# A graph layer on one core: y of a block made from its own x and placed by a selection product, and the first five parts gathering rows of x while the table is built

## The chip, the core and the metric

The program runs on one core of one Trainium2 chip. A core has TensorE (PE; the loads of its stationary operand are listed apart as PEld), VectorE (DVE), ScalarE (ACT), GpSimd (POOL) and SyncE (SP). Each works through its own list of instructions in order; they wait for one another through semaphores. DMAs are issued here from SP, ACT and POOL. The metric is the device time of the whole program in microseconds (us), as the median of several executions.

## What is computed

```python
N, D = 12500, 128                      # nodes, features
E = 412500                             # edges, sorted by dst
theta = x[dst] - x[src]
w = sigmoid(relu(theta @ W1 + b1) @ W2 + b2)      # one weight per edge
agg = segment_sum(w * theta, dst, num_segments=N)
indeg = segment_sum(ones(E, 1), dst, num_segments=N)
gnn = agg + indeg * (x @ W4 + b4)
out = layernorm(x + gnn)               # eps 1e-5
```

All inputs and the output are fp32. With y = x W1, an edge needs relu(y[dst] - y[src] + b1); the sum w * (x[dst] - x[src]) needs the row x[src] as well.

## The kernel before

**The table.** For all nodes the kernel first computes y = x W1 and stores rows z = [y | x] of 256 numbers (1 KB) in DRAM. This loop (L122 to L142) runs over 14 chunks, 12 of them of 1024 nodes: load x (L127, ACT's queue), transpose 128 x 128 tiles on TensorE (L133), copy them to SBUF (L135), multiply by W1 (L138), copy y into the tile `zt` (L140), copy x beside it (L141), store `zt` to z (L142, SP's queue). `zt` has three buffers, `xt` six.

**The parts.** The edges are cut in parts of 1024 (8 tiles of 128 edges): 403 parts, the last with 7 tiles. For each tile POOL issues one indirect DMA that gathers the 128 rows z[src] into `zbuf` (L233); there are 3223 of them. `zbuf` has 7 buffers, and the gather of part s+4 stands in the program at part s. `src_i` holds the indices; it is made by loading the edge list, transposing it on TensorE and converting it (`place_src`, L297).

**The blocks.** Two parts make a block (202 blocks). The 96 nodes from the first dst of a block are its window; a part's own window is 41 nodes from the part's first dst. For each block SP loads x of the window (`xw`, L343) and, for each of its parts, the 41 rows y three times, one below the other, into `yw` (L336: six DMAs of 20.5 KB per block from z; `yw` has three buffers). Rows 123 to 125 of `yw` hold b1 in three pieces. `window` (L346) splits y into three bf16 pieces, so that a product in bf16 is exact enough: ACT L351 makes `yh`, ACT L352 copies `yw` into PSUM, DVE L353 and ACT L355 make the second piece, DVE L357 writes `y3`. It also transposes `xw` (PE L359, ACT L361 gives `xwT`).

**A part's work.** `one_hots`: TensorE copies the dst offset of every edge over all partitions (PE L372, into the single PSUM buffer `pd`, in two halves of 4 tiles), DVE L375 turns each half into a selection matrix `oh`, PE L379 multiplies it with `y3` and so puts y[dst] + b1 of every edge into PSUM (`ph`). DVE L382 builds the second selection matrix `ow` (edge to node of the window; two buffers). `weights`: DVE L393 subtracts y[src] out of `zbuf`, DVE L394 applies relu and the factor W2, DVE L398 sums to one number `lg` per edge, ACT L399 takes the sigmoid, and eight ACT instructions L401 scale the rows x[src] into `wx`. `add_up`: eight fp32 matmuls PE L419 add `ow`^T `wx` into the block's sum `pa`; before the first of them PE L415 brings over the sum of nodes shared with the block before. At a block's end `total` reads `pa` (ACT L439 into `a`), computes x W4 + b4 (PE L442 and L443) and the row of the layer norm (DVE L450 to L457), and `store` writes rows that are done (DVE L429, SP L430). Every eighth block the square root is taken for eight blocks at once (ACT L462, with a table load before it and one after).

**The order.** SP's instructions run as the program lists them (`manual_schedule`). On the other engines a scheduler has fixed the order when the kernel was built. For a block, counted from its first part, "even", and its second, "odd", VectorE's list before the change is: L393 odd; L382 odd; L450; L394 even; L451; L398 even; L453; L353; L375 (second half, next even); small ones; L375 (first half, next odd); L357; L382 next even; L394 odd; L375 (second half, next odd); L398 odd; L393 next even; L375; and then L393 of the next odd part.

Two small PSUM pools matter here: `ps_l` has one buffer each for `pd`, `pw` and `pa`, and `ps_h` has two for `ph`.

Of the kernel before, what the change touches and what calls it, by code (L numbers as in the profile page):

```python
# [30 lines left out]
LB = 8  # L31
EPS = 1e-5
# [3 lines left out]
def gnn_resnorm(  # L36
# [12 lines left out]
):  # L49

# [67 lines left out]

    with tc.tile_pool(name="tab", bufs=3) as tp, tc.tile_pool(
        name="tab_ps", bufs=2, space=bass.MemoryType.PSUM  # L120
    ) as tps:
        for n0, np_, m in chunks:  # L122
            def rows_of(t):
                return t[n0:n0 + np_ * m, :].rearrange("(p t) d -> p t d", t=m)

            xt = tp.tile([P, TC, D], F32, name="xt", bufs=6)
            nc.scalar.dma_start(xt[:np_, :m, :], rows_of(x))  # L127
            zt = tp.tile([P, TC, 2 * D], F32, name="zt")
            for g0 in range(0, m, G):
                g = min(G, m - g0)  # L130
                px = tps.tile([P, G, P], F32, name="tpx")
                for j in range(g):
                    nc.tensor.transpose(px[:, j, :np_], xt[:np_, g0 + j, :], ident[:np_, :np_])  # L133
                xT = tp.tile([P, G, P], F32, name="txT")
                nc.scalar.activation(xT[:, :g, :np_], px[:, :g, :np_], AF.Copy)  # L135
                py = tps.tile([P, G, D], F32, name="tpy")
                for j in range(g):
                    nc.tensor.matmul(py[:np_, j, :], xT[:, j, :np_], wts[:, 0, :],  # L138
                                     start=True, stop=True)
                nc.vector.tensor_copy(zt[:np_, g0:g0 + g, :D], py[:np_, :g, :])  # L140
            nc.scalar.activation(zt[:np_, :m, D:], xt[:np_, :m, :], AF.Copy)  # L141
            nc.sync.dma_start(rows_of(z), zt[:np_, :m, :])  # L142

    base_r = const.tile([1, NS], I32, name="base_r")
    with nc.allow_non_contiguous_dma(reason="each part's first dst"):
        nc.scalar.dma_start(
            base_r, bass.AP(tensor=dst.tensor, offset=dst.offset, ap=[[0, 1], [BE, NS]]))
    loaded.append(load(nc.scalar, dst, *sets[0]))
    nc.scalar.dma_start(wts[:, 1, :], W4)
    rows = {}  # L150
    for name, v in (("b4_r", b4), ("b1_r", b1), ("w2_r", W2)):
        rows[name] = const.tile([P, D], F32, name=name)
        nc.scalar.dma_start(
# [3 lines left out]
    nc.scalar.dma_start(b2_c, bass.AP(tensor=b2.tensor, offset=b2.offset, ap=[[0, P], [1, 1]]))  # L157
# [25 lines left out]
    y_f = fix[:, 2 * P:].rearrange("p (h d) -> p h d", h=SUB)  # L183
# [19 lines left out]
    nc.vector.scalar_tensor_tensor(place_c, ge[3], -4.0 * N, place_c, op0=OP.mult, op1=OP.add)  # L203
    b1_s = const.tile([P, D], F32, name="b1_s")
    bh = const.tile([P, D], BF16, name="bh")
    br = const.tile([P, D], F32, name="br")
    e_c = const.tile([P, 1], F32, name="e_c")
    nc.vector.tensor_copy(br, b1_r)
    nc.vector.memset(b1_s, 0.0)
    for lo, hi in zip([ge[3]] + eb[:2], eb):  # L210
        nc.vector.tensor_copy(bh, br)
        nc.vector.tensor_sub(e_c, lo, hi)
        nc.vector.scalar_tensor_tensor(b1_s, bh, e_c, b1_s, op0=OP.mult, op1=OP.add)
        nc.vector.tensor_sub(br, br, bh)

    yw_buf = [const.tile([P, SUB, D], F32, name=f"yw{i}") for i in range(3)]
    for t in yw_buf:
        nc.vector.memset(t, 0.0)
        for h in range(SUB):
            nc.vector.tensor_copy(t[96:, h, :], b1_s[96:, :])  # L220
# [10 lines left out]
    def gather(s):  # L231
        for k in range(tiles(s)):
            nc.gpsimd.indirect_dma_start(  # L233
                out=zbuf[s % NZ][:, k, :], out_offset=None, in_=z,
# [3 lines left out]
    base_s = const.tile([1, NS], I32, name="base_s")  # L238
# [81 lines left out]
    with tc.manual_schedule(engines={SP}), tc.tile_pool(name="work", bufs=2) as wp, tc.tile_pool(  # L320
# [163 lines left out]
        for s in range(min(AHEAD, NS)):  # L484
            gather(s)
# [215 lines left out]
```

## Time and profile before

| | |
|---|---|
| median of 10 runs | 4125.93 us (4121.54 to 4127.70) |
| the profiled execution | 4122.61 us, of which its span from the first to the last instruction is 4120.8 us |
| TensorE clock granted, mean over the span | 0.657 of full speed |
| busy: PE, PEld | 2567.9 us (62%), 2111.3 us (51%) |
| busy: DVE | 2812.6 us (68%) |
| busy: ACT | 1507.9 us (37%) |
| busy: POOL | 3049.0 us (74%) |
| DMA | 494.31 MB, mean 120 GB/s; 369 GB/s in the first 40 us |

A busy share is a mean over the span. Between 80 and 4090 us the kernel repeats itself every 20 us, one block at a time, so the shares say how full each engine is within a block, and the idle time before an instruction, with what ended it, says what that instruction waited for. Times in a timeline are us from the start of the span. In it, a row is one instruction or several of one line merged: start, duration, engine, line, operation, output<-inputs, shape, count, and in brackets the idle time of the engine before it with what ended it. Durations of matmuls are modelled, and an fp32 matmul leaves two records.

### The profile page before, as it was taken

What the parts mean: (1) busy time and instruction counts of PE and PEld (TensorE: products, weight loads), DVE (VectorE), ACT (ScalarE), POOL (GpSimd) and SP (SyncE); (2) the same over time, 40 slices, a digit from 0 to 9 for tenths busy, and PEclk for the clock granted to TensorE, in tenths of its full rate; (3) what the DMA queues carried; (4) which work ended last, traced back from release to release, by engine and by line L of the source; (5) the groups of instructions that cost most, each with busy time, mean ns of one, the idle gap of its engine ahead of it and who ended that gap; (6) DMA issues with size and microseconds to landing.
All of it is one profiled execution on the core that took longest, in us unless ns stands there. A gap on an engine that the chain in (4) does not pass through costs nothing.

```text
span 4120.8 us, 54409 instructions
## 1 busy us (share of the span) xinstructions
PE 2567.9 (62%) x14665; PEld 2111.3 (51%) x14665; DVE 2812.6 (68%) x4456; ACT 1507.9 (37%) x4782; POOL 3049.0 (74%) x3232
## 2 busy tenths in 40 slices
PE   5666656666656566566666666666566666666665
PEld 4555545545545445455555555555444555545554
DVE  5777667667667667666666676676676676676666
ACT  4343333333333333333333333333333333333333
POOL 3777777777777777777777777777777777777775
PEclk8666666667666676766676666666766666666665
DMA  7443444444444434444444444444344344444442
GB/s 267 116 118 114 121 116 115 119 116 117 118 114 120 117 113 121 116 114 121 116 115 119 117 116 117 116 119 118 113 120 117 113 122 116 114 120 116 116 119 85
DMA packets 257189, 494.31 MB, mean 120 GB/s; under 512 B 60441, under 2 KB 149858, under 8 KB 255336
## 3 DMA queue, kind: packets, MB, share of 16 engines
q0 software_dynamic: 154704, 422.65, 35.9%
q1 hardware_dynamic: 98284, 58.66, 4.8%
q10 hardware_dynamic: 3884, 9.44, 0.6%
q8 instruction: 118, 1.93, 0.2%
q14 instruction: 199, 1.63, 0.1%
HBM read 467.78 MB, written 22.73 MB: 119 GB/s over the span
## 4 chain that ended last, share of the span: by engine, by line
DVE 28%; DMA 28%; ACT 15%; PE 13%; issue 11%; POOL 4%; SPq 1%; DVEq 0%; ACTq 0%; POOLq 0%
DMA zbuf<-z,src_i 26%; ACT wx L401 12%; PE pa L419 11%; DVE lg L398 10%; DVE h L394 7%; DVE ow L382 5%; POOL zbuf L233 4%; ACT wx L399 3%; DVE oh L375 2%; DVE h L393 2%; PE pd L372 1%; DVE v L451 1%; DMA z<-zt 1%; DVE y L357 1%; DVE o L429 1%
## 5 line engine op out<-in xcount | busy, mean ns | idle before, releaser
L233 POOL DMA_INDIRECT zbuf<-z,src_i x3223 | 3047.9, 946 | 1042.8 <-issue 511.4
L419 PE MATMUL pa<-wx,ow 128*96 128x130 f32 x6446 | 1597.2, 414 | 206.6 <-ACT wx L401 188.0
L419 PEld LDWEIGHTS pa<-wx,ow 128*96 128x96 f32 x6446 | 1286.8, 259 | 444.4 <-ACT wx L401 363.6
L401 ACT ACTIVATE wx<-zbuf,wx 128x128 f32<-128x128 f32 x3223 | 988.3, 388 | 13.2
L375 DVE TENSOR_SCALAR oh<-pd,place_c,one_c 128x512 bf16<-128x512 f32 x806 | 646.3, 802 | 508.0 <-PE pd L372 508.0
L393 DVE TENSOR_TENSOR h<-ph,zbuf 128x1024 f32<-128x1024 f32 x403 | 491.1, 1219 | 534.5 <-DMA zbuf<-z,src_i 527.5
L372 PE MATMUL pd<-ident_b,off 128*128 128x128 bf16 x3223 | 668.8, 284 | 150.8 <-DVE oh L375 146.3
L415 PE MATMUL pa<-a,sh 96*96 96x130 f32 x402 | 130.3, 422 | 807.5 <-DVE v L451 806.5
L399 ACT ACTIVATE wx<-lg,b_c 128x8 f32<-128x8 f32 x403 | 124.1, 308 | 1366.7 <-DVE lg L398 1361.3
L415 PEld LDWEIGHTS pa<-a,sh 96*96 96x96 f32 x402 | 71.1, 231 | 860.4 <-issue 858.5
L394 DVE SCALAR_TENSOR_TENSOR h<-h,fix 128x1024 f32<-128x1024 f32 x403 | 486.9, 1208 | 0.0
L398 DVE TENSOR_REDUCE lg<-h 128x8 f32<-128x1024 f32 x403 | 486.9, 1208 | 0.0
L379 PE MATMUL ph<-y,oh 128*128 128x128 bf16 x3223 | 348.8, 274 | 213.9 <-DVE oh L375 213.7
L372 PEld LDWEIGHTS <-off 128*128 128x128 bf16 x3223 | 389.5, 136 | 107.3 <-issue 94.3
L382 DVE TENSOR_TENSOR ow<-fix,rel 128x768 f32<-128x768 f32 x403 | 383.1, 951 | 75.3 <-PE pa L419 75.2
L379 PEld LDWEIGHTS <-oh 128*128 128x128 bf16 x3223 | 278.2, 125 | 261.8 <-DVE oh L375 253.0
L352 ACT ACTIVATE fix<-yw 128x256 f32<-128x256 f32 x202 | 78.2, 387 | 593.3 <-DVE h L394 593.3
L351 ACT ACTIVATE yh<-yw 128x256 bf16<-128x256 f32 x202 | 82.7, 409 | 271.0 <-DMA yw<-z 271.0
L359 PE MATMUL pw<-ident,xw 96*128 96x96 f32 x202 | 85.0, 421 | 142.1 <-DVE v L453 129.3
L439 ACT ACTIVATE a<-pa 96x130 f32<-96x130 f32 x202 | 55.4, 274 | 313.4 <-PE pa L419 313.4
L429 DVE TENSOR_SCALAR o<-v,mv,sd 96x128 f32<-96x128 f32 x202 | 63.8, 353 | 125.3 <-DMA out_dram<-o 125.1
L359 PEld LDWEIGHTS pw<-ident,xw 96*128 96x128 f32 x202 | 36.7, 182 | 207.1 <-DVE v L453 193.4
(96 smaller groups left out, 1280.2 us busy)
## 6 DMA issues: line engine op xcount, KB each, us to landing
zbuf<-z,src_i POOLq DMA_INDIRECT x3223
yw<-z SPq DMA_DIRECT2D x1209, 20.5 KB
z<-zt SPq DMA_DIRECT2D x12, 1024.0 KB
xw<-in_x_dram SPq DMA_DIRECT2D x202, 48.0 KB
out_dram<-o SPq DMA_DIRECT2D x202, 48.0 KB
xt<-in_x_dram ACTq DMA_DIRECT2D x12, 512.0 KB
e_i<-in_dst_dram ACTq DMA_DIRECT2D x3, 512.0 KB
e_i<-in_src_dram ACTq DMA_DIRECT2D x2, 512.0 KB
```

The source lines that it names most:

```text
L233: nc.gpsimd.indirect_dma_start(out=zbuf[s % NZ][:, k, :], out_offset=None, in_=z, in_offset=IndirectOffsetOnAxis(ap=src_i[:, k, s:s + 1], ...
L372: nc.tensor.matmul(pd[:, j, :], off[:, k0 + j, s:s + 1].to_broadcast([P, P]), ident_b, start=True, stop=True)
L375: nc.vector.tensor_scalar(oh[:, k0:k0 + g, :], pd[:, :g, :], place_c, one_c, op0=OP.is_equal, op1=OP.max)
L379: nc.tensor.matmul(ph[:, k, :], oh[:, k, :], blocks[b]["y3"][:, h, :], start=True, stop=True)
L382: nc.vector.tensor_tensor(ow[:, :n, :], iota_f.to_broadcast([P, n, WB]), rel[:, :n, s:s + 1].to_broadcast([P, n, WB]), op=OP.is_equal)
L393: nc.vector.tensor_sub(h[:, :n, :], d["ph"][:, :n, :], zs[:, :n, :D])
L394: nc.vector.scalar_tensor_tensor(h[:, :n, :], h[:, :n, :], 0.0, w2_f.to_broadcast([P, n, D]), op0=OP.max, op1=OP.mult)
L398: nc.vector.tensor_reduce(lg[:, :n], h[:, :n, :], AX.X, OP.add)
L399: nc.scalar.activation(wx[:, :n, D], lg[:, :n], AF.Sigmoid, bias=b2_c)
L401: nc.scalar.activation(wx[:, k, :D], zs[:, k, D:], AF.Copy, scale=wx[:, k, D:D + 1])
L415: nc.tensor.matmul(bd["pa"][:WB], sh[:WB, :WB], carry[0][:WB], start=True, stop=False)
L419: nc.tensor.matmul(bd["pa"][:WB], d["ow"][:, k, :], wx_buf[s % 2][:, k, :], start=h == 0 and k == 0 and carry[0] is None, stop=end and k = ...
```

## The change

Y of a block's window is no longer loaded. TensorE multiplies the transposed `xw` by W1 (new L360, into the PSUM tile `pw`), ACT copies the result to SBUF (`yb`, L362; rows 96 to 98 hold b1's three pieces, written once), and for each of the two parts a selection matrix `pick` (DVE L367, from the constants `behind` and `far`) puts the rows at their places in a product (PE L370, into `pw`). From there `yh`, `y1`, `ym`, `y3` follow as before, reading PSUM. The loads L336 and their register loads go.

Parts 0 to 4 (`NH = 5`) gather rows of x, not of z, into the x half of `zbuf`, so they need no table; their y[src] is computed in `both`: transposes of the gathered rows, and a product with -W1 on top of the product with `y3`. Their gathers stand ahead of the table in the program. The table moves into the main pools: its PSUM tiles are now `pd`, `pw` and `ph`, `zt` has two buffers and `xt` four, and y is copied 1024 columns at a time. The first loads of dst, of the b and W rows and of the first two `xw` move from ACT's queue, or from behind the table, to SP's queue ahead of the table's stores. The later conversions of edge lists (`turns`) come at parts 16, 22, 28 and so on, in place of 8, 11, 14. The tile `pw` is now a whole PSUM bank, still with one buffer.

```diff
@@ ahead of the main loop @@
-    with tc.tile_pool(name="tab", bufs=3) as tp, ...
-        for n0, np_, m in chunks:
...
-        nc.scalar.dma_start(
+        nc.sync.dma_start(
             base_r, bass.AP(tensor=dst.tensor, offset=dst.offset, ap=[[0, 1], [BE, NS]]))
-    loaded.append(load(nc.scalar, dst, *sets[0]))
-    nc.scalar.dma_start(wts[:, 1, :], W4)
+    loaded.append(load(nc.sync, dst, *sets[0]))
...
+    behind = const.tile([P, P], F32, name="behind")
+    nc.vector.memset(behind, -4.0)
+    for i in range(3):
+        nc.vector.tensor_copy(behind[:WB, i * SW:(i + 1) * SW], lag[:WB, :SW])
...
+    far = const.tile([P, NS], F32, name="far")
+    nc.vector.tensor_sub(far, first_c, base_cs[:, :NS])
+    nc.vector.memset(far[WB:, :], 0.25)
@@ gather @@
+            z_k = zbuf[s % NZ][:, k, :]
             nc.gpsimd.indirect_dma_start(
-                out=zbuf[s % NZ][:, k, :], out_offset=None, in_=z,
+                out=z_k if s >= NH else z_k[:, D:], out_offset=None, in_=z if s >= NH else x,
@@ main loop: loads @@
-        def load_part(s):
-            base = nc.values_load(base_s[0:1, s:s + 1], engines=[SP], ...)
-            b, h = divmod(s, SUB)
-            for i in range(3):
-                nc.sync.dma_start(
-                    yw_buf[b % 3][i * SW:(i + 1) * SW, h, :], z[ds(base, SW), :D])
+        def table_load(c):
+            n0, np_, m = chunks[c]
+            xt = tp.tile([P, TC, D], F32, name="xt", bufs=4)
+            nc.scalar.dma_start(xt[:np_, :m, :], ...)
+            return xt
+        def table_chunk(c, xt):
+            n0, np_, m = chunks[c]
+            zt = tp.tile([P, TC, 2 * D], F32, name="zt")
+            py = ps_h.tile([P, K, D], F32, name="ph")
+            for g0 in range(0, m, G):
+                g = min(G, m - g0)
+                px = ps_l.tile([P, G, P], F32, name="pw" if g0 else "pd")
+                for j in range(g):
+                    nc.tensor.transpose(px[:, j, :np_], xt[:np_, g0 + j, :], ident[:np_, :np_])
+                xT = tp.tile([P, G, P], F32, name="txT")
+                nc.scalar.activation(xT[:, :g, :np_], px[:, :g, :np_], AF.Copy)
+                for j in range(g):
+                    nc.tensor.matmul(py[:np_, g0 + j, :], xT[:, j, :np_], wts[:, 0, :],
+                                     start=True, stop=True)
+            nc.vector.tensor_copy(zt[:np_, :m, :D], py[:np_, :m, :])
+            nc.scalar.activation(zt[:np_, :m, D:], xt[:np_, :m, :], AF.Copy)
+            nc.sync.dma_start(z[n0:n0 + np_ * m, :]..., zt[:np_, :m, :])
@@ window @@
-            yw = yw_buf[b % 3]
-            yh = wp.tile([P, SUB, D], BF16, name="yh")
-            nc.scalar.activation(yh, yw, AF.Copy)
-            nc.scalar.activation(y_f, yw, AF.Copy)
-            nc.vector.scalar_tensor_tensor(y_f, yh, m12, y_f, op0=OP.mult, op1=OP.add)
...
             nc.scalar.activation(xwT[:, :WB], pw[:, :WB], AF.Copy)
+            pw = ps_l.tile([P, G, P], F32, name="pw")[:, 0, :]
+            nc.tensor.matmul(pw[:WB], xwT[:, :WB], wts[:, 0, :], start=True, stop=True)
+            yb = yb_buf[b % 2]
+            nc.scalar.activation(yb[:WB], pw[:WB], AF.Copy)
+            ns = min(SUB, NS - b * SUB)
+            py = ps_l.tile([P, G, P], F32, name="pw")[:, :ns, :]
+            for h in range(ns):
+                pick = wp.tile([P, P], F32, name="pick")
+                nc.vector.tensor_scalar(pick[:YB], behind[:YB],
+                                        far[:YB, b * SUB + h:b * SUB + h + 1], None,
+                                        op0=OP.is_equal)
+                nc.tensor.matmul(py[:, h, :], pick[:YB], yb[:YB], start=True, stop=True)
+            yh = wp.tile([P, SUB, D], BF16, name="yh")
+            nc.scalar.activation(yh[:, :ns, :], py, AF.Copy)
+            y1 = fix[:, 2 * P:].rearrange("p (h d) -> p h d", h=SUB)[:, :ns, :]
+            nc.vector.scalar_tensor_tensor(y1, yh[:, :ns, :], m12, py, op0=OP.mult, op1=OP.add)
...
@@ parts 0 to 4 @@
+        def both(s):
+            d = parts[s]
+            b, h = divmod(s, SUB)
+            for k0 in range(0, K, G):
+                px = ps_l.tile([P, G, P], F32, name="pw")
+                for j in range(G):
+                    nc.tensor.transpose(px[:, j, :], zbuf[s % NZ][:, k0 + j, D:], ident)
+                xT = tp.tile([P, G, P], F32, name="txT")
+                nc.scalar.activation(xT, px, AF.Copy)
+                for j in range(G):
+                    ph = d["ph"][:, k0 + j, :]
+                    nc.tensor.matmul(ph, d["oh"][:, k0 + j, :], blocks[b]["y3"][:, h, :],
+                                     start=True, stop=False)
+                    nc.tensor.matmul(ph, xT[:, j, :], wneg, start=False, stop=True)
@@ order of the program @@
+        fetch(0)
+        fetch(1)
+        xts = [table_load(0), table_load(1)]
         place_src(0, ps_l, loaded[0])
+        for s in range(AHEAD):
+            gather(s)
+        for c in range(len(chunks)):
+            if c + 2 < len(chunks):
+                xts.append(table_load(c + 2))
+            table_chunk(c, xts.pop(0))
         place_dst(0, ps_l, loaded[1])
-        for s in range(min(AHEAD, NS)):
-            gather(s)
-        fetch(0)
         prepare(0)
-        fetch(1)
```

The scheduler's order for the changed kernel, for a block in the steady state, is part of the change. TensorE: L397 (was L379) 16 times; L460 (was L419) 8 times for the odd part; L390 (was L372) 4 times; L456 (was L415); L356 (was L359); L460 8 times for the even part with four L390 among them; **L360**; L390 4 times; **L370 twice**; L390 4 times; L483 and L484 (were L442, L443); and L397 again. ScalarE: eight L442 (was L401) of the even part; L358 (was L361); **L362**; L372; L376; then L440 (was L399) and eight L442 of the odd part; L480 (was L439). VectorE: L434 odd (was L393); L400 odd (was L382); L491; L435 even (was L394); L492; L439 even (was L398); L494; L393 (was L375); small ones; L393 twice for the next odd part; **L367**; L374; **L367**; L378 (was L357); L400 next even; L435 odd; L434 next even; L439 odd; L393; and L434 of the next odd part.

## The prediction

> **What bounds it now.** I read the costliest groups first, then the gather line's own listing:
>
> ```profile
> L233 POOL DMA_INDIRECT zbuf<-z,src_i x3223 | 3047.9, 946 | 1042.8 <-issue 511.4
> L393 DVE TENSOR_TENSOR h<-ph,zbuf 128x1024 f32<-128x1024 f32 x403 | 491.1, 1219 | 534.5 <-DMA zbuf<-z,src_i 527.5
> L351 ACT ACTIVATE yh<-yw 128x256 bf16<-128x256 f32 x202 | 82.7, 409 | 271.0 <-DMA yw<-z 271.0
> ```
> ```profile
> L233 POOL DMA_INDIRECT zbuf<-z,src_i x3223: 942/946/1098, 63.1 to 4091.5; - x190
> ```
>
> POOL starts a gather every (4091.5 - 63.1) / 3222 = 1.2503 us: 0.946 of work and 0.30 between two. VectorE waits 527.5 us for gathered rows, ScalarE 271.0 for `yw`. Does POOL ever wait in earnest? Its busy time in a window of 1000 us:
>
> ```profile
> 1000.00:2000.00 1000.00, 615.78 (x3550) 505.51 (x3550) 682.93 (x1055) 361.86 (x1168) 756.30 (x801) 0.67 0.41 117
> ```
>
> The fifth number is POOL's: 801 gathers, so 1.25 us each, as over the whole run. POOL is the bound: 16 gathers, 20.0 us, per block. How far behind it are the others? In the VectorE timeline of an early block the gathers are ahead (127.55 waits for PE, not for rows), so its length is that of the consumers alone:
>
> ```profile
> 111.36 1.21 DVE L398 TENSOR_REDUCE lg<-h 128x8 f32<-128x1024 f32 x1
> 118.10 0.47 DVE L357 SCALAR_TENSOR_TENSOR y<-ym,m,fix 128x256 bf16<-128x256 bf16 x1
> 121.21 1.21 DVE L398 TENSOR_REDUCE lg<-h 128x8 f32<-128x1024 f32 x1
> 127.55 0.96 DVE L382 TENSOR_TENSOR ow<-fix,rel 128x768 f32<-128x768 f32 x1 [1.53 <-PE pa L419]
> 129.87 1.21 DVE L398 TENSOR_REDUCE lg<-h 128x8 f32<-128x1024 f32 x1
> ```
>
> From lg even (ends 112.57) to the next lg even (131.08) is 18.51. It is a ring with four pieces: (a) to y3's end, 118.57: 6.0; (b) to lg odd's end, 122.42: 3.85; (c) to the start of `ow`, which needs lg odd's sigmoid, eight scalings and eight `pa` products: 5.13; (d) to lg even's end: 3.53. Over the 67 blocks where `ow` waited for `pa` the ring is 16.8 to 18.5 us long, 17.95 at the median of those with no write of results and no square root in them. So only 1.5 to 3.2 us per block stand between the consumers and POOL's 20.0. What happens when y3 is late shows once the write of results holds VectorE up:
>
> ```profile
> 2032.13 1.21 DVE L398 TENSOR_REDUCE lg<-h 128x8 f32<-128x1024 f32 x1
> 2040.43 0.37 DVE L429 TENSOR_SCALAR o<-v,mv,sd 96x128 f32<-96x128 f32 x1 [5.03 <-DMA out_dram<-o]
> 2041.41 0.47 DVE L357 SCALAR_TENSOR_TENSOR y<-ym,m,fix 128x256 bf16<-128x256 bf16 x1
> 2052.70 1.21 DVE L398 TENSOR_REDUCE lg<-h 128x8 f32<-128x1024 f32 x1
> ```
>
> y3 ended 8.54 after lg even (2041.88 - 2033.34) and that block took 20.57; the 22 such blocks average 8.67 and 20.98. POOL outlived it only because most blocks are shorter.
>
> The start: z's 14 stores are issued over 46.61 us, the last lands at 62.11, and the first gather starts at 63.1.
>
> ```profile
> 10.73 46.61 SPq L142 DMA_DIRECT2D z<-zt  x14
> ...
> ```
> ```profile
> 56.16 5.95 DMA z<-zt
> ```
>
> **Removed.** Six `yw` loads a block and their 271.0 us of ScalarE waits. ScalarE is idle 63% of the span and the ring does not pass through the wait, so this gives 0 unless the loads hold back other DMAs: 0 to 0.3 us a block off the ring. With them, SP's queue is free for the rows that are stored, so part of the wait ahead of `o` goes (125 us in all, 0.6 a block); where the new y3 is late anyway, it hides that wait, so I count 0.
>
> **Added to the ring, in piece (a).** Before, y3 was made while TensorE did the even part's `pa`; only VectorE's order placed it at 6.0. Now TensorE's order has L360 behind those eight products, and TensorE got there 5.17 us after lg even (117.75 - 112.57; 1014.90 - 1009.73 in another block):
>
> ```profile
> 117.75 0.45 PE L442 MATMUL pw<-b_r,ones_r 1*96 1x128 f32 x2
> 118.14 0.46 PE L443 MATMUL pw<-wts,xwT 128*96 128x128 f32 x2
> ```
>
> From there all is serial across three engines. Prices by rows: L360 as L443, 0.46 (0.74 where the granted clock is 0.50); `yb` as L439's copy, 0.28; the two picks as the pair L442 and L443, 0.85 (1.41); `yh` as L351, 0.41; y1 as L353, 0.47; `ym` as L355, 0.36; y3 as L357, 0.47; six hand-overs at 0.05, as between neighbours in the rows: 0.30. Sum 3.6, or 4.4 at half clock. Reading PSUM in place of SBUF in `yh` and y1 is not in the trace for those shapes; from 0.1 faster to 0.3 slower each, between L355's and L353's rows; I take them as they are. y3 ends at 5.18 + 3.6 = 8.8 (9.6 at half clock), in place of 6.0.
>
> The two `pick` comparisons (L413's 96x96 row has 0.24) and VectorE's idle time before y3 fit together: they cost 0, and 0.5 if VectorE were late. The single `pw` buffer passes through five hands, all in this chain and counted. L483 and L484 wait behind y1 for `pw`; next in TensorE's list is `ph`, which y3 holds up longer, so 0; without that cover 0.85.
>
> **Piece (b)**: y3 is followed by `ow` 0.87, relu odd 1.12, the subtraction of the next even part 1.13 (moved ahead), lg odd 1.13: 4.25, where it was 3.85. **Piece (c)**: the odd `pa` products lose three `pd` matmuls between them, 3 x 0.11; 5.04 at the median becomes about 4.5 (3.4 with the full clock, 4.8 with half throughout). **Piece (d)** keeps its order: 3.53.
>
> **The ring** is 8.8 + 4.25 + 4.5 + 3.53 = 21.1 us. At half clock throughout 9.6 + 4.25 + 4.8 + 3.53 = 22.2; with the clock up midway through `pa`, 8.0 + 4.25 + 3.4 + 3.53 = 19.2. POOL needs 20.0. I take 21.1: the row at 117.75 has the full clock just there, and the 22 late blocks (8.67 and 20.98) are its measured neighbour.
>
> The clock decides. It is granted in steps:
>
> ```profile
> 101.00:102.00 1.00, 0.62 (x8) 0.45 (x8) 1.00 (x2) 0.16 (x1) 0.69 (x2) 1.00 0.48 144
> 102.00:103.00 1.00, 0.00 (x0) 0.00 (x0) 1.00 (x2) 0.67 (x3) 0.90 (x1) 1.00 0.46 139
> 103.00:104.00 1.00, 0.91 (x7) 0.77 (x7) 1.00 (x2) 1.00 (x5) 0.80 (x1) 1.00 0.42 111
> 104.00:105.00 1.00, 1.00 (x8) 0.93 (x7) 0.28 (x2) 1.00 (x4) 0.70 (x2) 0.56 0.34 90
> ```
>
> The last column but two is the clock: it fell to half in 104:105, although the three microseconds before had PE (first of the busy numbers) 0.62, 0.00 and 0.91 busy. The chain for y3 leaves TensorE nearly as empty, so it will mostly be at half when `pa` begins. The Trainium skill ("TensorE: Matmul & The Clock Gate", Part 1, What's actually happening) has it otherwise: the clock falls only after a whole idle window of about 3.4 us. By that rule the changed ring, which has no such gap, would stay at full clock, piece (a) 5.17 - 1.7 + 3.6 = 7.0, the ring 7.0 + 4.25 + 3.42 + 3.53 = 18.2, and POOL would remain the bound; the row, with half a window busy, says it falls.
>
> **The start.** POOL now waits only for `src_i`: the load, the transposes, and ScalarE's conversion, which stands behind a copy that needs `w2_r`. On rows of before (a load lands in about 6 us; `b_r` took 6.36) that is 12, bounds 9 and 20. 40 gathers of x cover 50 us. The table's first store waits for TensorE's `pd` tile, some 18 in place of 10.73; with 46.61 of issuing and 6 to land that is 71. The 40 gathers bring 40 x 64 KB = 2.6 MB more, 7 us at the 369 GB/s of the first 40 us, if the DMAs are the limit there: 78. I take 73, with 63 (as before) and 90 (two `zt` buffers in place of three) as bounds. Gather 41 starts there, where it was 63.1 + 50.0 = 113.1: POOL is 40 us ahead. Parts 0 to 4 each pay 16 fp32 transposes and products more in `both`: 16 x 0.25 (L419's spacing at the full clock) = 4.0, less the subtraction that falls away, 1.13, and some 1.4 beside VectorE's work: 1.5 a part, 2.5 for each of three blocks. The first lg even, at 89.0 before, comes near 84.
>
> **Sums.** If POOL stays the bound: 73 + 3182 x 1.2503 + 29.3 (last gather's start to the span's end, as before) + 1.8 (4122.61 - 4120.8) = 4083. If the ring is the bound, POOL's head start fills `zbuf` and then waits: 84 + three blocks of 21.1 + 2.5 (71) + 198 x 21.1 + 17.0 (last lg to the end) + 1.8 = 4350, exactly 4348 with 21.08. The profiled run stands 3.3 below the median; I leave it there. 0.2%, about 8 us, is what a measurement of this kernel can tell from no change.
>
> **Rivals.**
> 1. *POOL stays the bound, the head start is kept: 4083.* For it: 1.5 to 3.2 us of slack, and TensorE gets more work and so perhaps more clock. Against: the price of 2.8 in (a) and 0.4 in (b) is over the slack at the median. It decides where the ring is under 19.9. 21%.
> 2. *A tie:* ring 19.8 to 20.3; 4083 to 4190. 10%.
> 3. *The head start is not had* (x gathers and table share the DMAs so that z is no earlier usable, POOL bound): 4123. For it: DMA is full between 5 and 50 us. 4%.
> 4. *All at half clock:* 22.2 a block, 84 + 71 + 198 x 22.2 + 18.8 = 4570. It needs the clock never up at 5.2 us into a block; the row at 117.75 is against. 7%.
> Forecast, the ring at 20.4 to 21.9: 58%, own range 4210 to 4510. On the other side of it stands rival 1, faster.
>
> Faster: rival 1 and a fifth of the tie, 0.23. Same: rival 3, 0.04. Slower: 0.73. The range goes from rival 1 with a slightly earlier table (4070) to a ring of 21.8 (4490); 12 in 100 are above it, 5 below.
>
> **What would show it.** Gathers: mean spacing over 1.25 from block 3 on, POOL's busy share down to 71%. L434's wait for `zbuf` near none; instead L378 (y3) or L400 waits on ScalarE and PE. y3's end 8.8 after lg even, the ring 21.1; L360 5.2 after lg even. First x gather near 12, first z gather near 73. Wrong if gathers keep 1.2503 to the end (rival 1), if the first z gather is past 100 (rival 3), or if L360 runs ahead of `pa` or the clock is 1.00 through the chain.

## The result, and the profile after

The changed kernel takes 4339.88 us at the median of 8 runs, against 4125.83 us before: a ratio of 1.0518, 95% interval 1.0509 to 1.0527. It is 5.2% slower. The profiled execution took 4331.5 us, its span 4329.7. The forecast was 4348.

Which resource ends the waits now? The costliest groups of the changed kernel (line, engine, operation, tiles, count; busy us and mean ns; idle time before them and what ended it):

```profile
L218 POOL DMA_INDIRECT zbuf<-z,src_i x3183 | 3010.1, 946 | 1183.9 <-issue 575.0
L400 DVE TENSOR_TENSOR ow<-fix,rel 128x768 f32<-128x768 f32 x403 | 384.4, 954 | 514.4 <-PE pa L460 514.3
L434 DVE TENSOR_TENSOR h<-ph,zbuf 128x1024 f32<-128x1024 f32 x398 | 484.2, 1217 | 0.7 <-PE ph L397 0.7
L362 ACT ACTIVATE yb<-pw 96x128 f32<-96x128 f32 x202 | 55.1, 273 | 470.7 <-PE pw L360 470.7
```

VectorE's 527.5 us of waits for gathered rows are gone (L434 has 0.7, and not for rows). In their place `ow` waits 514.4 us for `pa`, where it had 75.2, and the new copy `yb` waits 470.7 us for the product L360. The gathers cost 946 ns each as before; there are fewer in the same time, 766 in place of 801 in the window of 1000 us:

```profile
1000.00:2000.00 1000.00, 625.55 (x3683) 523.45 (x3681) 691.44 (x1106) 348.17 (x1113) 723.21 (x766) 0.67 0.37 106
```

16 gathers a block at 766 in 1000 us are 20.9 us a block. One ring in the VectorE timeline:

```profile
1016.19 1.21 DVE L439 TENSOR_REDUCE lg<-h 128x8 f32<-128x1024 f32 x1
...
1023.01 0.81 DVE L393 TENSOR_SCALAR oh<-pd,place_c,one_c 128x512 bf16<-128x512 f32 x1 [0.88 <-PE pd L390]
...
1024.27 0.49 DVE L374 SCALAR_TENSOR_TENSOR fix<-yh,m,pw 128x256 f32<-128x256 bf16 x1 [0.26 <-ACT yh L372]
...
1025.21 0.48 DVE L378 SCALAR_TENSOR_TENSOR y<-ym,m,fix 128x256 bf16<-128x256 bf16 x1 [0.21 <-ACT ym L376]
...
1028.74 1.21 DVE L439 TENSOR_REDUCE lg<-h 128x8 f32<-128x1024 f32 x1
...
1034.60 0.96 DVE L400 TENSOR_TENSOR ow<-fix,rel 128x768 f32<-128x768 f32 x1 [2.80 <-PE pa L460]
...
1036.92 1.21 DVE L439 TENSOR_REDUCE lg<-h 128x8 f32<-128x1024 f32 x1
```

An end is a row's start plus its duration, here as in the prediction. From lg even (ends 1017.40) to the next (1038.13) it is 20.73. y3 ends at 1025.69, so piece (a) is 8.29; (b) to lg odd's end at 1029.95 is 4.26; (c) to `ow` at 1034.60 is 4.65; (d) is 3.53. No row in between waits for gathered data. The chain to y3, in the timelines of TensorE and of ScalarE:

```profile
1022.37 0.38 PE L360 MATMUL pw<-wts,xwT 128*96 128x128 f32 x2
...
1023.11 0.71 PE L370 MATMUL pw<-yb,pick 99*128 99x128 f32 x4
```
```profile
1022.78 0.27 ACT L362 ACTIVATE yb<-pw 96x128 f32<-96x128 f32 x1 [2.44 <-PE pw L360]
1023.86 0.38 ACT L372 ACTIVATE yh<-pw 128x256 bf16<-128x256 f32 x1 [0.80 <-PE pw L370]
1024.80 0.38 ACT L376 ACTIVATE ym<-fix 128x256 bf16<-128x256 f32 x1 [0.56 <-DVE fix L374]
```

Each instruction waits for the one before it on another engine: L360 at 1022.37, `yb`, picks, `yh`, y1 at 1024.27, `ym`, y3 at 1025.21: 3.32 us from L360's start to y3's end.

The start, in POOL's and in SP's timeline:

```profile
14.57 1.10 POOL L218 DMA_INDIRECT zbuf<-in_x_dram,src_i  x1 [12.80 <-ACT src_i L286]
...
63.40 0.94 POOL L218 DMA_INDIRECT zbuf<-in_x_dram,src_i  x1 [0.30 <-issue]
82.59 0.94 POOL L218 DMA_INDIRECT zbuf<-z,src_i  x1 [18.25 <-DMA xw<-in_x_dram]
```
```profile
22.77 56.11 SPq L342 DMA_DIRECT2D z<-zt  x14
```

The x gathers begin at 14.57 and end near 65; the first gather from z is at 82.59, where the 41st gather before the change was at about 113. So the head start is there, 30 us of it, and still the kernel is slower.

### The profile page after: what moved, and what is told of

The parts are those of the page before. It is cut to its first block, busy times and chain, and to the rows that moved or that the text cites. A ratio compares the mean times of both kernels' runs of the same rounds, so it can differ in the third digit from the quotient of the medians.

```text
span 4329.7 us, 52854 instructions
## 1 busy us (share of the span) xinstructions
PE 2716.6 (63%) x15995; PEld 2275.7 (53%) x15995; DVE 2954.0 (68%) x4841; ACT 1525.4 (35%) x4792; POOL 3049.2 (70%) x3232
## 5 line engine op out<-in xcount | busy, mean ns | idle before, releaser
L218 POOL DMA_INDIRECT zbuf<-z,src_i x3183 | 3010.1, 946 | 1183.9 <-issue 575.0
L460 PE MATMUL pa<-wx,ow 128*96 128x130 f32 x6446 | 1600.5, 426 | 683.6 <-ACT wx L442 667.8
L460 PEld LDWEIGHTS pa<-wx,ow 128*96 128x96 f32 x6446 | 1354.7, 273 | 813.6 <-ACT wx L442 764.8
L393 DVE TENSOR_SCALAR oh<-pd,place_c,one_c 128x512 bf16<-128x512 f32 x806 | 648.3, 804 | 613.2 <-PE pd L390 596.1
L442 ACT ACTIVATE wx<-zbuf,wx 128x128 f32<-128x128 f32 x3223 | 988.0, 388 | 13.2
L400 DVE TENSOR_TENSOR ow<-fix,rel 128x768 f32<-128x768 f32 x403 | 384.4, 954 | 514.4 <-PE pa L460 514.3
L440 ACT ACTIVATE wx<-lg,b_c 128x8 f32<-128x8 f32 x403 | 124.1, 308 | 1588.6 <-DVE lg L439 1588.6
L390 PE MATMUL pd<-ident_b,off 128*128 128x128 bf16 x3223 | 540.6, 271 | 127.5 <-DVE oh L393 114.7
L439 DVE TENSOR_REDUCE lg<-h 128x8 f32<-128x1024 f32 x403 | 487.0, 1208 | 0.0
L434 DVE TENSOR_TENSOR h<-ph,zbuf 128x1024 f32<-128x1024 f32 x398 | 484.2, 1217 | 0.7 <-PE ph L397 0.7
L435 DVE SCALAR_TENSOR_TENSOR h<-h,fix 128x1024 f32<-128x1024 f32 x398 | 480.8, 1208 | 0.0
L390 PEld LDWEIGHTS <-off 128*128 128x128 bf16 x3223 | 357.4, 127 | 183.0 <-issue 160.4
L456 PE MATMUL pa<-a,sh 96*96 96x130 f32 x402 | 127.1, 413 | 438.1 <-DVE v L492 437.1
L456 PEld LDWEIGHTS pa<-a,sh 96*96 96x96 f32 x402 | 69.5, 226 | 482.6 <-issue 481.2
L397 PE MATMUL ph<-y,oh 128*128 128x128 bf16 x3183 | 242.5, 236 | 23.3 <-DVE oh L393 5.6
L397 PEld LDWEIGHTS <-oh 128*128 128x128 bf16 x3183 | 220.3, 106 | 59.0 <-issue 50.2
L362 ACT ACTIVATE yb<-pw 96x128 f32<-96x128 f32 x202 | 55.1, 273 | 470.7 <-PE pw L360 470.7
L480 ACT ACTIVATE a<-pa 96x130 f32<-96x130 f32 x202 | 55.6, 275 | 363.0 <-PE pa L460 363.0
L483 PE MATMUL pw<-b_r,ones_r 1*96 1x128 f32 x404 | 91.5, 306 | 134.7 <-DVE fix L374 134.7
L367 DVE TENSOR_SCALAR pick<-behind,far 99x128 f32<-99x128 f32 x403 | 125.5, 322 | 71.7 <-PE pw L370 71.4
L370 PE MATMUL pw<-yb,pick 99*128 99x128 f32 x806 | 151.8, 313 | 21.4 <-ACT yb L362 2.2
L356 PE MATMUL pw<-ident,xw 96*128 96x96 f32 x202 | 81.3, 402 | 131.2 <-DVE v L494 131.2
```

What stands on the lines that cost most here:

```text
L218: nc.gpsimd.indirect_dma_start(out=z_k if s >= NH else z_k[:, D:], out_offset=None, in_=z if s >= NH else x, in_offset=IndirectOffsetOnAxi ...
L370: nc.tensor.matmul(py[:, h, :], pick[:YB], yb[:YB], start=True, stop=True)
L390: nc.tensor.matmul(pd[:, j, :], off[:, k0 + j, s:s + 1].to_broadcast([P, P]), ident_b, start=True, stop=True)
L393: nc.vector.tensor_scalar(oh[:, k0:k0 + g, :], pd[:, :g, :], place_c, one_c, op0=OP.is_equal, op1=OP.max)
L397: nc.tensor.matmul(ph[:, k, :], oh[:, k, :], blocks[b]["y3"][:, h, :], start=True, stop=True)
L400: nc.vector.tensor_tensor(ow[:, :n, :], iota_f.to_broadcast([P, n, WB]), rel[:, :n, s:s + 1].to_broadcast([P, n, WB]), op=OP.is_equal)
```

## The experiments

Medians; each is compared with the kernel before on the same chip, which took 4124.74 to 4124.87 us in all of them, so times of different runs can be set side by side to about 1 us. Ring lengths and pieces are read from the VectorE timeline over the 197 blocks from the fourth on, as above.

**Is the ring the bound? Two more steps in its chain.**

```diff
-            nc.scalar.activation(yb[:WB], pw[:WB], AF.Copy)
+            for i in range(2):
+                yc = wp.tile([P, D], F32, name=f"yc{i}")
+                nc.scalar.activation(yc[:WB], pw[:WB], AF.Copy)
+                pw = yc
+            nc.scalar.activation(yb[:WB], pw[:WB], AF.Copy)
```

> The changed kernel with two more ScalarE copies between `pw` and `yb`, which lengthen nothing but the chain to y3. Theory (the ring through y3 is the bound): each copy adds 0.28 and a hand-over of 0.05 to every block, 0.65 a block, 198 blocks, +129 us: about 4469, between 4440 and 4490; the ring 21.6. Rival (the time is lost at the start, or to more work on the engines as a whole): ScalarE is idle 65% of the span, so 4340 within 10.

Measured 4499.88 us, ratio 1.0912 (1.0893 to 1.0930): 160 us more than the changed kernel, and 10 us above the expected range. The chain's new steps in ScalarE's timeline:

```profile
1017.90 0.27 ACT L364 ACTIVATE yc<-pw 96x128 f32<-96x128 f32 x1 [2.76 <-PE pw L360]
1018.21 0.31 ACT L364 ACTIVATE yc<-yc 96x128 f32<-96x128 f32 x1
1018.55 0.31 ACT L366 ACTIVATE yb<-yc 96x128 f32<-96x128 f32 x1
```

The two copies add 0.65 from the first `yc` to `yb`, as expected, and all of it comes through: the median ring goes from 20.76 to 21.57. The mean ring, 21.81 against 20.97, gained 0.85, which is 0.2 more than the copies. The mean clock fell from 0.675 to 0.636: the even `pa` products ran wholly at half clock in 133 of the 197 blocks, against 87 in the changed kernel. Among such blocks alone piece (a) grew by 0.69, so most of the 0.2 goes with the clock. Work on an engine that is idle 65% of the span lengthens the kernel when it lies in the ring.

**Or do the early gathers cost?** All gathers from z, behind the table:

```diff
-NH = 5
+NH = 0
...
-        for s in range(AHEAD):
-            gather(s)
         for c in range(len(chunks)):
...
         place_dst(0, ps_l, loaded[1])
+        for s in range(AHEAD):
+            gather(s)
```

> The changed kernel with all gathers from z, behind the table (NH = 0); y of a block still made from its x. Theory: the ring stays 20.97; the first gather at about 82, the first lg even at about 101, 101 + 201 x 20.97 + 18.8 = 4335, between 4320 and 4350: the 40 us of head start are worth next to nothing. Rival (the early gathers or `both` are what costs): about 4125 plus the 19 us by which the table is later, 4145.

Measured 4331.11 us, ratio 1.0505 (1.0487 to 1.0522). The rival is out: without early gathers the loss stays. The ring is 20.97 again. And the head start is not only worth little: lg even of the fourth block ends at 167.1 without it and at 168.0 with it. Without it POOL started at 80.08 and a block took 20.4 from the second on (126.4 to 167.1 for two); with it part 0's lg ended at 93.1, but the three blocks to 168.0, whose first five parts go through `both`, took 25 each.

**Only the loads of y back.** The six loads a block, the tiles `yw` and the old `window`, in the changed kernel:

```diff
-            nc.tensor.matmul(pw[:WB], xwT[:, :WB], wts[:, 0, :], start=True, stop=True)
-            yb = yb_buf[b % 2]
...
+            yw = yw_buf[b % 3]
+            nc.scalar.activation(yh, yw, AF.Copy)
+            nc.scalar.activation(y_f, yw, AF.Copy)
...
+                nc.sync.dma_start(
+                    yw_buf[b % 3][i * SW:(i + 1) * SW, h, :], z[ds(base, SW), :D])
```

> The changed kernel with the six loads of y per block back in place of the selection product; the early gathers stay. Theory: the ring is as before the change, about 18 us, POOL the bound at 20.0 a block, and the start is the changed one: 4083 to 4105, the first blocks with `both` deciding where. Rival (the early gathers cost): above 4130. Rival (the new ring is not from the y chain): 4340.

Measured 4113.93 us, ratio 0.9972 (0.9962 to 0.9982). y3 ends at 6.0 again, the window of 1000 us has 801 gathers, so the 226 us between this kernel and the changed one are the selection product's. It is 9 us above the range: POOL's timeline shows three waits for the consumers' first blocks (showing only the gathers from 85 us on that waited more than 2 us):

```profile
85.42 0.94 POOL L212 DMA_INDIRECT zbuf<-z,src_i  x1 [20.00 <-DMA yw<-z]
...
114.26 0.94 POOL L212 DMA_INDIRECT zbuf<-z,src_i  x1 [9.13 <-ACT wx L432]
...
142.75 0.94 POOL L212 DMA_INDIRECT zbuf<-z,src_i  x1 [8.81 <-ACT wx L432]
...
168.83 0.94 POOL L212 DMA_INDIRECT zbuf<-z,src_i  x1 [6.38 <-ACT wx L432]
```

The first row is the wait for z (18.25 in the changed kernel); the other three add up to 24 us. The first `yw` loads stand behind the table's stores on SP's queue, the first parts are late, and POOL, with all seven buffers filled, waits for them.

**All of the change's work, in another order.** In the changed kernel L356, which begins the chain, waits 131.2 us for VectorE's L494, since `pw` has one buffer and L494 reads x W4 + b4 out of it behind lg even. Give that product the spare columns of the bank of `pa`:

```diff
-            pu = ps_l.tile([P, G, P], F32, name="pw")[:, 0, :]
+            pu = pa[:, 2 * D:3 * D]
...
-                bd["pa"] = ps_l.tile([P, AW], F32, name="pa")
+                bd["pa"] = ps_l.tile([P, G * P], F32, name="pa")
```

> The changed kernel with the product x W4 + b4 in the spare half of the bank of `pa`, so that `pw` serves the y chain alone. The scheduler then starts the chain a block earlier: the picks stand behind the `ph` products of the block before, y1 directly behind lg even, y3 ahead of `ow`. All the added work stays. Theory (the chain counts only because it is serial behind the even `pa`): y3 ends about 6 after lg even, the ring is 18 to 19, POOL the bound: 4083 to 4125. Rival (the added work on TensorE, VectorE and ScalarE, or a slower clock, sets the ring wherever it stands): above 4250.

Measured 4093.39 us, ratio 0.9929 (0.9913 to 0.9946): with this one edit 0.7% faster than the kernel before. In its VectorE timeline (lg even ended at 1001.09):

```profile
1001.26 0.47 DVE L374 SCALAR_TENSOR_TENSOR fix<-yh,m,pw 128x256 f32<-128x256 bf16 x1
...
1005.32 0.47 DVE L378 SCALAR_TENSOR_TENSOR y<-ym,m,fix 128x256 bf16<-128x256 bf16 x1
...
1016.36 1.23 DVE L434 TENSOR_TENSOR h<-ph,zbuf 128x1024 f32<-128x1024 f32 x1 [4.88 <-DMA zbuf<-z,src_i]
```

y1 follows lg even with one small row between, since its picks were made in the block before; y3 ends 4.7 behind lg even, and VectorE waits 4.88 for gathered rows: POOL is the bound again, 800 gathers in 1000 us. The products, the picks and the copies are all still there; only their place differs. The mean clock rose to 0.730, but not where the old chain waited: the even `pa` products ran wholly at half clock in 105 of the 197 blocks, more than the 87 of the changed kernel.

**Shorter chains.** Two kernels that leave work out of it; both compute something else (the added copy on ScalarE fills the columns of `xwT` that the wider products read):

```diff
-            nc.tensor.matmul(pw[:WB], xwT[:, :WB], wts[:, 0, :], start=True, stop=True)
-            yb = yb_buf[b % 2]
-            nc.scalar.activation(yb[:WB], pw[:WB], AF.Copy)
+            nc.scalar.activation(xwT[:, WB:], pw[:, :P - WB], AF.Copy)
...
-                nc.tensor.matmul(py[:, h, :], pick[:YB], yb[:YB], start=True, stop=True)
+                nc.tensor.matmul(py[:, h, :], xwT, wts[:, 0, :], start=True, stop=True)
```

> The changed kernel without `yb` and the picks: two products xwT^T W1 go directly to the two halves of `pw`, so y is not put at the places of the part's nodes, the sums are those of other rows, and b1 is left out; all later steps stay. The chain loses L360 with its hand-over, `yb` 0.28 and a hand-over: 0.8. Theory (slope 1 while the ring is over 20.0): ring 20.2, time 4340 - 0.8 x 198 = 4182 (4150 to 4210). Rival (ring not the bound, or POOL already): 4340, or 4100 at once.

> As the kernel without `yb` and picks, and also without `ym` and the third piece: y3 is written straight by the step of y1, in bf16, so y is rounded to fewer digits. Another 0.36 + 0.47 + 0.05 = 0.9 off the chain: ring 19.3. Theory: POOL's 20.0 takes over, and the time stops at 4090 to 4125, not at 4340 - 1.7 x 198 = 4003. Rival (the ring alone sets the time): 4003 to 4030.

Measured 4310.13 us, ratio 1.0453 (1.0436 to 1.0471), for the first: 30 us gained, not 158, and 9 of them before the fourth block (its lg even ends at 159.2, not 168.0); the mean ring lost only 0.09. The theory as it stood has failed here. 4101.70 us, ratio 0.9939 (0.9923 to 0.9956), for the second, on POOL's floor as expected (the scheduler also put y3 behind `ow` there, which helps). What held the first up, in the timelines of TensorE and VectorE:

```profile
1015.46 1.06 PE L363 MATMUL pw<-wts,xwT 128*128 128x128 f32 x4
1016.32 0.50 PE L383 MATMUL pd<-ident_b,off 128*128 128x128 bf16 x4
```
```profile
1016.85 0.81 DVE L386 TENSOR_SCALAR oh<-pd,place_c,one_c 128x512 bf16<-128x512 f32 x1 [1.69 <-PE pd L383]
1017.58 0.48 DVE L367 SCALAR_TENSOR_TENSOR fix<-yh,m,pw 128x256 f32<-128x256 bf16 x1
```

y1 starts the moment `oh` is done, and `oh` waited for `pd`, which TensorE makes behind the two products. In the changed kernel VectorE went on from `oh` at 1023.74, only 0.53 ahead of y1 at 1024.27, so a second way through the ring lies close behind the chain. To test that, one product in place of two, so that `pd` is not held up:

```diff
-            for h in range(ns):
-                nc.tensor.matmul(py[:, h, :], xwT, wts[:, 0, :], start=True, stop=True)
+            nc.tensor.matmul(pw[:, 0, :], xwT, wts[:, 0, :], start=True, stop=True)
+            py = pw[:, 0:1, :].to_broadcast([P, ns, P])
```

> The kernel without `yb` and picks once more, with one product in place of two (both parts read the same half of `pw`; again y is not placed and b1 left out). In the kernel with two products y1 came no earlier, since `oh` stands ahead of it in VectorE's list and waited 1.69 for `pd`, which stood behind the second product. If that is the cause of its small gain, `pd` is as early as in the changed kernel, where `oh` ended 0.53 ahead of y1: the ring loses 0.5, 4235 (4200 to 4260). Rival (nothing but the chain counts): 1.1 less, 4122. Rival (the chain does not count at all): 4310 as with two products.

Measured 4232.33 us, ratio 1.0272 (1.0253 to 1.0291), against 4235. `oh` then sets y1 from 0.5 below:

```profile
1006.27 0.81 DVE L386 TENSOR_SCALAR oh<-pd,place_c,one_c 128x512 bf16<-128x512 f32 x1 [1.14 <-PE pd L383]
1007.00 0.48 DVE L367 SCALAR_TENSOR_TENSOR fix<-yh,m,pw 128x256 f32<-128x256 bf16 x1
```

**The clock.** TensorE products repeated, with the same result, in the stretches where TensorE waits:

```diff
-                for j in range(g):
+                for j in list(range(g)) * (5 if h == 0 and k0 == 0 and s >= NH else 1):
                     nc.tensor.matmul(
                         pd[:, j, :], ...
...
-            for k in range(n if s >= NH else 0):
+            for k in list(range(n if s >= NH else 0)) * (4 if h == 1 else 1):
                 nc.tensor.matmul(ph...
```

> The changed kernel with TensorE products repeated that give the same result again: the odd part's `ph` four times in place of one, and the first four `pd` products of an even part five times; 40 more products a block, of which most fall into the time in which TensorE waits for `wx` or for y3. Nothing else changes. If the granted clock follows how empty TensorE is in the microseconds before (as the rows of before had it), it is up more of the time, pieces (a) and (c) lose up to 1.7 and 1.2 us, the ring is 18.2 to 20.5 and the time 4095 to 4250 in spite of more work. Rival (the clock does not turn on that, or the added products delay the ring more than the clock gives): 4340 or more.

Measured 4314.56 us, ratio 1.0457 (1.0440 to 1.0475); the mean clock rose from 0.675 to 0.778. Half of the expected showed: piece (c), where the gap had been filled, fell from 4.65 to 3.38 at the median; piece (a) did not fall (8.68, from 8.33), since the scheduler had put the other repeats behind L360, most of them behind the picks, and left the gap ahead of the even `pa`. The median hides that (c) fell only in 122 of 197 blocks, whose ring is 19.76 in the mean; in the other 75 the clock was down in the odd `pa` all the same, (c) was mostly 5.1 to 5.3 and the ring 22.67. So the mean ring is 20.87, hardly under 20.97. By windows of 1 us (PE busy, granted clock, DMA share, GB/s) of this kernel, around the gap:

```profile
1000.00:1001.00 1.00, 0.22 (x4) 1.00 0.31 74
1001.00:1002.00 1.00, 0.00 (x0) 1.00 0.24 90
1002.00:1003.00 1.00, 0.42 (x2) 1.00 0.49 131
1003.00:1004.00 1.00, 0.14 (x2) 0.74 0.59 152
1004.00:1005.00 1.00, 0.90 (x4) 0.50 0.65 177
```

So the repeats of `pd` were moved into that gap (`7 if h == 1 and k0 == 0` in place of `5 if h == 0 and k0 == 0`):

> As the kernel with repeated products, but the `pd` repeats (24) stand where TensorE waits ahead of the even part's `pa`, and the `ph` repeats (24) ahead of the odd part's as there. In the run before, the granted clock was 0.50 in the even `pa` after microseconds with TensorE 0.22, 0.00, 0.42 and 0.14 busy, and piece (c) had fallen to 3.38 where the gap was filled. If filling the other gap holds the clock at 1.00 too, piece (a) loses 1.7 as well, the ring is near 18 and POOL the bound: 4090 to 4160. Rival (the clock falls there all the same, or the filling delays `pa`): 4290 or more.

Measured 4111.17 us, ratio 0.9973 (0.9958 to 0.9987): 229 us less than the changed kernel, with 48 products more in every block and the chain at its old place. Its windows show the full clock from the odd `pa` through the gap into the even one:

```profile
1012.00:1013.00 1.00, 1.00 (x11) 1.00 0.38 98
1013.00:1014.00 1.00, 1.00 (x14) 1.00 0.34 82
1014.00:1015.00 1.00, 1.00 (x22) 1.00 0.24 82
1015.00:1016.00 1.00, 0.25 (x5) 1.00 0.49 139
1016.00:1017.00 1.00, 0.43 (x2) 1.00 0.47 131
1017.00:1018.00 1.00, 0.30 (x1) 1.00 0.47 139
```

Mean clock 0.845, y3 at 6.5 behind lg even in half of the blocks, mean ring 19.85, and VectorE waits for gathered rows again in 91 blocks. In most of the others y3 stands near 8.0; in the one that begins at 1017 the clock fell in the middle of the even `pa`, at 1019.4. That the clock does it, and not the new order, shows within this one kernel: in the 113 of 197 blocks whose even `pa` ran wholly at 1.00 piece (a) is 6.51 at the median, and in the 79 in which the clock changed on the way it is 8.01.

**What the early gathers are worth when POOL is the bound.** The kernel with its own place for x W4 + b4, with `NH = 0` and the gathers behind the table, edited as above:

> The kernel with the product x W4 + b4 in the bank of `pa`, with all gathers from z, behind the table (NH = 0). Theory: POOL is the bound, so each microsecond of head start counts: first gather at about 84, 84 + 3222 x 1.2506 + 27 + 3 = 4143 (4130 to 4150), 50 us more than with the early gathers. Rival (the early gathers are worth nothing in this kernel either, as between the changed kernel and the one with NH = 0): 4093.

Measured 4138.34 us, ratio 1.0032 (1.0021 to 1.0044). First gather at 83.40, last at 4112.8. With early gathers it was 4093.39: 45 us, where the kernel bound by the ring gave nothing.

**A version that beats both kernels.** `NH = 6`, and with it more loads of x at the start:

```diff
-            xt = tp.tile([P, TC, D], F32, name="xt", bufs=4)
+            xt = tp.tile([P, TC, D], F32, name="xt", bufs=5)
...
-        xts = [table_load(0), table_load(1)]
+        xts = [table_load(c) for c in range(4)]
...
-            if c + 2 < len(chunks):
-                xts.append(table_load(c + 2))
+            if c + 4 < len(chunks):
+                xts.append(table_load(c + 4))
```

> The kernel with the product x W4 + b4 in the bank of `pa`, with six parts gathered from x in place of five (NH = 6). POOL stood 19 us idle between the last x gather and the first z gather there. Theory: 8 gathers more are done in that time, but part 7 waits for the buffer of part 0, at about 97 in place of 104: 7 us less, 4086. Rival (a sixth part through `both` holds the consumers up): 4093 or more.

> The same with four loads of x issued at the start and five buffers for them (`o_f` has one buffer to make room). DMA moved only 91 to 226 GB/s between 10 and 25 us in the kernel before, against some 370 later, so up to 8 us of the table's time can go. Theory: the consumers start earlier by as much: 4078 (4074 to 4086). Rival (the table is not what sets POOL's start any more, or the loads hold up the first x gather): no change, 4086.

Measured 4090.06 us, ratio 0.9916 (0.9903 to 0.9930), and 4088.55 us, ratio 0.9917 (0.9904 to 0.9931). Both are faster than the kernel before by 0.8%. Against `NH = 5` (0.9929) and against each other the intervals overlap, so no gain of these two steps is shown; the 8 us of the second did not come. The first z gather came at 82.71 in the profile of the second, 86.72 in that of the first, 83.99 with `NH = 5`.

## Why the prediction was right

**The bound before** was read rightly: 20.0 us of POOL a block, consumers 1.5 to 3.2 us below it. That slack is the one of blocks without a write of results; those that waited to write results, and whose `ow` waited for `pa` as well, took 20.2 to 21.7 us. The three kernels that put y3 early, or the ring's clock up, without touching the gathers all come back to 800 gathers in 1000 us.

**The ring** was forecast as 8.8 + 4.25 + 4.5 + 3.53 = 21.1. Measured medians: 8.33, 4.26, 4.65 and 3.53, whole ring 20.76, mean 20.97. So piece (a) was over by almost 0.5 and (c) under by 0.15. The serial chain was mis-sized by 0.27: from L360 to y3's end 3.33 at the median in place of 3.6, since from L360's start to that of `yb` it was 0.42 (0.46 + 0.05 forecast) and from the picks to `yh` 0.75 (0.85 + 0.05). L360 started 4.98 after lg even, forecast 5.17. The mean came nearer to 21.08 than the median by a term that the forecast did not have: every eighth block, with its square root, takes 22.30 us, the others 20.78. That was luck.

That this chain is the cause is shown from three sides: longer by 0.65 it costs 160 us, made a block earlier it costs nothing, and with y loaded again in its place the cost is gone. It needs the half clock beside it: with the chain at its old place and TensorE's gaps filled, 4111.17 us. So either remedy alone, the chain moved or the gaps filled, brings the time back to POOL's or near it.

**Costs put at nothing.** The two picks, VectorE's idle time before y3, L483 and L484, and the removed ScalarE waits: none appears in the ring, as forecast. What the text did not see is the `oh` path: the picks and the chain hide `pd` and `oh`, which are next, 0.53 below. So what stands ahead of y1 in the chain could not have won back more than 0.5 by being shorter, as the kernel with one product showed; the steps behind y1 are not hidden by `oh`, and without `ym` and the third piece the time was at POOL's floor, partly by the new place of y3.

**The clock decides**: the row was right and the rule was not. The prediction set the Trainium skill's rule ("TensorE: Matmul & The Clock Gate", Part 1, What's actually happening: the clock falls after a whole idle window) against a row where it fell after a half-busy stretch. The changed kernel's windows (PE busy, granted clock, DMA share, GB/s), between `ph` and the odd `pa`:

```profile
1026.00:1027.00 1.00, 0.80 (x15) 1.00 0.22 70
1027.00:1028.00 1.00, 0.00 (x0) 1.00 0.34 115
1028.00:1029.00 1.00, 0.00 (x0) 1.00 0.47 131
1029.00:1030.00 1.00, 0.00 (x0) 0.55 0.43 123
```

A mean of 0.55 in the last of them puts the fall near 1029.1, after some 2.3 us of idle time, and both sets of `pa` products then ran at 0.50. (The prediction also had it that the changed ring has no gap as long as 3.4 us; TensorE stood idle for 3.98 us here, but the clock fell before 3.4 of them were over.) In the windows of the repeated products above it fell although 0.42 and 0.14 of two of the microseconds before were busy. By the rule the prediction's sum came to 4083; the time was 4339.88, and the kernel with the gaps filled, where the clock does stay up, is at 4111.17. The estimate of a ring of 18.2 at the full clock was near: 17.7 to 18.8 is the length of the shortest fifth of that kernel's rings.

One sign that the prediction had named for being wrong did come: from L360 to y3 the clock was at 1.00 in 122 of 197 blocks, and at 0.50 all through in 3. The sign was ill chosen, since the sum itself prices the chain at the full clock; the half clock sits in the `pa` products, ahead of the chain and in piece (c).

**The start** was off in three terms. The first z store came at 22.77 (18 forecast), the stores took 56.11 and not 46.61, and the first z gather was at 82.59 (73, bounds 63 and 90): DMA was not at 369 GB/s all along; between 10 and 25 us of the changed kernel it moved 218 to 239 GB/s. The fourth block's lg even ended at 168.0, where 84 + 71 = 155 was forecast. The end was mis-sized too: from the last lg even of a full block (4298.05) to the span's end, with a last block of one part in it, it is 31.6, where 21.08 + 17.0 was forecast.

**The sum**, by measured terms: 168.0 + 197 x 20.97 + 31.6 + 1.8 = 4332, the profiled execution. Against 155 + 198 x 21.08 + 17.0 + 1.8 that is +13 at the start, -22 in 197 rings (0.11 each), -6 from there to the end. These errors cancel in part, so that the forecast of 4348 is only 8 above the median is partly luck; that the ring became the bound, and at about which length, is not.

**The rivals.** POOL staying the bound: the kernel in which it does stay so takes 4093, not 4083, by the later table. It failed here for the reason named, a ring over 19.9. The head start not had: false as worded, POOL was 30 us ahead at the 41st gather, but it was worth 0 under the ring and 45 without it. The tie and the ring at half clock throughout did not occur.

## What to carry to other kernels

When one engine bounds a loop with 10% of slack behind it, ask of each new operation not how long it is but whether it lies in the ring of waits that comes next; here 3.3 us of small serial steps on three engines, behind `pa` products at half clock, cost 5%, and the same steps cost nothing when one PSUM tile was given its own place so that the scheduler could start them a block earlier. A head start counts only while the resource that starts early stays the bound. Where TensorE's work comes in bursts, read the granted clock in microsecond windows: filling the gaps with repeated products gained 229 us in a kernel whose ring went through `pa`.

## What the runs showed of the hardware

The granted clock fell after stretches in which TensorE was partly busy, 0.22, 0.00, 0.42 and 0.14 of successive microseconds, and stayed at 1.00 over 0.25, 0.43 and 0.30 where full microseconds had come just before (from 1015 to 1018 in the kernel with the gaps filled; it fell at 1019.4).

The traces hold the clock more finely than windows of 1 us. In all fourteen of them the granted clock is 1.00 or 0.50 and changes only at whole multiples of 3.413 us from one another. In the changed kernel it rose at 1022.28, fell at 1029.11 and rose at 1042.76, that is 2 and 4 times 3.413 us apart:

```profile
1022.00:1023.00 1.00, 0.97 (x9) 0.86 0.32 102
...
1029.00:1030.00 1.00, 0.00 (x0) 0.55 0.43 123
...
1042.00:1043.00 1.00, 1.00 (x8) 0.62 0.23 61
```

Cut into such stretches, from 100 us to 5 us before its end, that trace has 267 falls, each after a stretch in which TensorE was busy for 0 to 0.76 of the time; in 9 of them it did nothing at all. The clock stayed up after stretches of 0.48 to 0.83 and rose after 0.79 or more. So a stretch need not be idle for the clock to fall, and the busy share alone does not decide it; what else counts stays open. That the same gap is harmless in one block and not in the next, as in the kernels with repeated products, may come from where it lies against these stretches; no run varied that.

The same fp32 products of `pa` followed one another about 0.30 us apart at the full clock in place of 0.59 at half, with a `pd` product between. Eight of them, with the four `pd` between, took 4.15 us in the changed kernel (1018.22 to 1022.37) and 2.35 where the gaps were filled (1000.41 to 1002.76). With the clock up, piece (a) was shorter by 1.8 us (8.33 at the median of the changed kernel, 6.51 in the blocks at 1.00 of the one with the gaps filled) and piece (c) by 1.3 (4.65 to 3.38, in the kernel with only that gap filled). Together that is nearly the length of the chain to y3. With both gaps filled the mean ring went from 20.97 to 19.85, next to the 20.0 that POOL needs.
